# Keys and values by seven quarter products in the middle groups of a gated decoder, and one buffer for the turned rows

## The chip, the cores and the metric

The kernel runs on one core of one Trainium2 chip. The metric is the device time of one execution in microseconds; the figure for the kernel before is the median of three runs. Everything is fp32.

## What is computed

Four batches (NB = 4) of 512 rows of 512 numbers go through two layers. Each layer adds a gated cross attention and a gated feed-forward part to x. The part that matters here is the cross attention of the second layer, cut from the reference:

```python
x = x + jnp.tanh(g_xattn[1]) * _L1_xattn_ref(_layernorm(x, axis=-1), ctx_1024, Wq, Wk, Wv, Wo, gq, gk)
# _L1_xattn_ref: 16 heads of D = 128, context of 512 rows of 256 numbers per batch
q = rmsnorm((hidden_states @ Wq).reshape(B, Sq, H, D), gq)
k = rmsnorm((encoder_hidden_states @ Wk).reshape(B, Skv, H, D), gk)
v = (encoder_hidden_states @ Wv).reshape(B, Skv, H, D)
attn = softmax(einsum('bqhd,bkhd->bhqk', q, k) / sqrt(D))
out = einsum('bhqk,bkhd->bqhd', attn, v).reshape(B, Sq, H * D) @ Wo
```

The first layer has another cross attention and a linear layer. The feed-forward part of the second layer is a mixture of 16 experts, applied to the first batch alone.

## The kernel before

**Groups and steps.** The second layer's attention is cut into 32 groups of two heads (G = 2), eight for each batch. `groups[m]` is the batch and the pair of group m. `step(i)` does head i of 64, so a group is two steps: h = 0 and h = 1. A step has four quarters. Each quarter starts with one score matmul (`scores(i, quarter)`, bank psS), and then issues what the lists `pieces` and `extra` hold for it. Group m's steps also make the keys, values and queries of group q = m + 1, and multiply the finished values and the output projection of earlier heads.

**The order of the work.** It is written out by hand. Each engine runs its instructions in the order in which the program issues them. `later(n, f)` puts f off until `tick` has counted n more units, where a 512-column matmul counts about one; so DVE and ACT work is issued between matmuls.

**Keys and values before.** `keys_values(q, chunks)` runs in the h = 0 step: in quarter 0 for two of four chunks of context rows, in quarter 1 for the other two. A chunk is two matmuls of 512 columns (keys and values of both heads side by side) into one bank psA, and ACT copies the halves to `kn` and `v`. Then, in the same function, come the squares of kn (ACT, L796), the mean and rsqrt (DVE L806, POOL L193), the scaling of kn (POOL L810), 32x32 transposes (DVE L821), and a way out to DRAM and back in another order (`k_d` L828 and `kT` L836), both issued on ACT's queue. `kT` is what the next group's first score matmul reads.

**Queries.** `queries` makes them by plain products (L858). For the groups `SWITCH[0] <= q < SWITCH[1]`, 12 to 27, `quarter_queries` makes them by seven products of quarters (L881): POOL combines the quarters of the weights (L731 to L734), and DVE the quarters of the turned rows once for a batch (`combine_rows`).

**Turned rows.** `turned_rows` gives the pieces that normalise a batch's rows (DVE, L227), transpose them on TensorE (L245, bank psT) and copy them to `lnT` (ACT, L250). For batches 1 to 3 its four statistics pieces start at step (b-1)*16 + 8, and its four turning pieces follow, one in quarter 3 of each of the next four steps. `lnT` has two buffers, which layer 0's `xTs` use as well.

**Beside it.** From step 22 on, the experts' blocks lie between the attention's pieces, one block for two steps: `rows_T` (L1133) in h = 0 quarter 0, the gate and up products (L1141) in quarters 1 and 2, and down (L1169) in h = 1 quarter 2. SP's queue loads all weights and moves the probabilities (`big<-tP`). The projections (L1066) and their adds to x (DVE L276) end a group. PSUM has eight banks: three psA, two psS, two psT, one psO.

Of the kernel before, what the change touches and what calls it, by code (L numbers as in the profile page):

```python
# [9 lines left out]
F32 = mybir.dt.float32  # L10
I32 = mybir.dt.int32
AF = mybir.ActivationFunctionType
ALU = mybir.AluOpType
AX = mybir.AxisListType

P = 128
NB = 4
S = 512
# [4 lines left out]
G = 2  # L23
NG = H // G
# [4 lines left out]
NC = S // P  # L29
KC = DM // P  # L30
# [3 lines left out]
SWITCH = (12, 28)  # L34
# [21 lines left out]
def tile_gated_decoder(  # L56
# [19 lines left out]
    nc = tc.nc  # L76
    const = ctx.enter_context(tc.tile_pool(name="const", bufs=1))
    work = ctx.enter_context(tc.tile_pool(name="work", bufs=2))
# [9 lines left out]
    def ps_a():  # L88
        return ps("psA", 3)
# [4 lines left out]
    def ps_t():  # L94
        return ps("psT", 2)
# [5 lines left out]
        return work.tile([P, 4, 512], F32, tag="big", bufs=2, name="big")  # L101

    def lnt():
        return work.tile([P, KC, S], F32, tag="lnT", bufs=2, name="lnT")

    def row(tag, bufs):
        return work.tile([P, 512], F32, tag=tag, bufs=bufs, name=tag)
# [10 lines left out]
    ctxs = {}  # L118
# [80 lines left out]
    def later(n, f):  # L199
        heapq.heappush(pending, (clock[0] + n, next(serial), f))  # L200

    def tick(n=1):
        clock[0] += n
        while pending and pending[0][0] <= clock[0]:
            heapq.heappop(pending)[2]()
# [138 lines left out]
    def l0_rows(b, c):  # L344

        if c == 0:
            xTs[b] = lnt()
        pt = ps_t()
        for k in range(KC):
            nc.tensor.transpose(  # L350
                pt[:, k * P : (k + 1) * P], x_sb[:, b * NC + c, k * P : (k + 1) * P], ident
            )
        later(0, lambda: nc.scalar.copy(
            xTs[b][:, :, c * P : (c + 1) * P], pt.rearrange("p (k q) -> p k q", k=KC)
        ))
        tick(0.5)
# [352 lines left out]

    HS, HK = S // 2, KC // 2

    def by_quarters(m):
        return SWITCH[0] <= m < SWITCH[1]
# [38 lines left out]
    def load_wo(m):  # L754
# [2 lines left out]
        nc.sync.dma_start(t, wo_v[:, g * G : (g + 1) * G, :])  # L757
        wo_of[m] = t

    def keys_values(m, chunks):  # L760


        b, wkv = groups[m][0], wkv_of[m]
        if m not in v_of:
            kn_of[m] = work.tile([P, NC, GD], F32, tag="kn", bufs=1, name="kn")
            v_of[m] = work.tile([P, NC, GD], F32, tag="v", bufs=3, name="v")
        kn, v = kn_of[m], v_of[m]

        def copies(c, pp):
            nc.scalar.copy(kn[:, c, :], pp[:, 0:GD])  # L770
            nc.scalar.copy(v[:, c, :], pp[:, GD : 2 * GD])  # L771

        for c in chunks:
            pp = ps_a()
            for k in range(CC):
                nc.tensor.matmul(  # L776
                    pp,
                    ctxs[b][:, k, c * P : (c + 1) * P],
                    wkv[:, k, :, :].rearrange("p a n -> p (a n)"),
                    start=(k == 0),  # L780
                    stop=(k == CC - 1),
                )
                tick()
            later(1, lambda c=c, pp=pp: copies(c, pp))
        if chunks[-1] < NC - 1:
            return
        st = {}

        def squares():
            st["kss"] = col(NC * G, "kss", 3)  # L790
            sq = work.tile([P, NC, GD], F32, tag="sq", bufs=1, name="ksq")

            def chunk(c):
                for h in range(G):
                    at = slice(h * D, (h + 1) * D)
                    nc.scalar.activation(  # L796
                        sq[:, c, at], kn[:, c, at], AF.Square,
                        accum_out=st["kss"][:, c * G + h : c * G + h + 1],
                    )

            for c in range(NC):
                later(c, lambda c=c: chunk(c))

        def scale():
            kss = st["kss"]
            nc.vector.tensor_scalar(kss, kss, 1.0 / D, EPS, ALU.mult, ALU.add)  # L806
            rk = col(NC * G, "rk", 3)
            rsqrt(rk, kss, NC * G)
            kn_v = kn.rearrange("p c (h d) -> p c h d", h=G)
            nc.gpsimd.tensor_tensor(  # L810
                kn_v, kn_v,
                rk.rearrange("p (c h) -> p c h", h=G).unsqueeze(3).broadcast_to([P, NC, G, D]),
                ALU.mult,
            )

        def turn():
            st["tK"] = work.tile([P, NT, G, NC, TB], F32, tag="tK", bufs=1, name="tK")
            for c in range(NC):  # L820
                nc.vector.transpose(  # L821
                    st["tK"][:, :, :, c, :].rearrange("p j h q -> p h j q"),
                    kn[:, c, :].rearrange("p (h j r) -> p h j r", h=G, r=TB),
                )

        def put_out():
            st["k_d"] = dram.tile([NT, TB, NT, G * P], F32, tag="k_d", bufs=2, name="k_d")
            nc.scalar.dma_start(  # L828
                st["k_d"].rearrange("t r j q -> (t r) (j q)"),
                st["tK"].rearrange("p j h c q -> p (j h c q)"),  # L830
            )

        def take_in():
            kT = work.tile([P, NT, G, P], F32, tag="kT", name="kT")
            for j in range(NT):
                nc.scalar.dma_start(  # L836
                    kT[j * TB : (j + 1) * TB].rearrange("r t h q -> r t (h q)"),
                    st["k_d"][:, :, j, :].rearrange("t r q -> r t q"),
                )
            k_of[m] = kT  # L840

        later(2, squares)
        later(6, scale)
        later(11, turn)
        later(14, put_out)
        later(18, take_in)
# [412 lines left out]
    def put(i, quarter, *fs):  # L1259
        extra.setdefault((i, quarter), []).extend(fs)  # L1260
# [19 lines left out]
    for b in range(1, NB):  # L1280
        i = (b - 1) * NG * G + NG
        for j, f in enumerate(turned_rows(b, lx1, lnt)):
            put(i + j // NC * (1 + j % NC), 3 if j >= NC else j, f)
        if (b + 1) * NG > SWITCH[0]:
            put(2 * max(b * NG, SWITCH[0]) - 2, 1, lambda b=b: combine_rows(b))
        if b > 1:
            put(i, 3, lambda b=b: load_ctx(b))

# [12 lines left out]
    def step(i):  # L1301
        m, h = divmod(i, G)
        q = m + 1
        late, late_before = by_quarters(q), by_quarters(m)
        pieces = [[], [], [], []]
        if i >= G:
            pieces[0 if i == n - 1 or h and late else 2].append(lambda: values(i - G))
        if i == n - 1:
            pieces[1].append(lambda: project(m - 1, [0, 1]))
            pieces[2] += [lambda: project(m - 1, [2, 3]), lambda: end_turn(0)]  # L1310
            pieces[3] += [lambda: values(i - 1), lambda: end_turn(1)]
            pieces[3] += [lambda: end_values(0), lambda: end_turn(2), lambda: end_values(1)]
            pieces[3] += [lambda: project(m, [0]), lambda: end_turn(3), lambda: end_values(2)]
            pieces[3] += [lambda: project(m, [1]), lambda: end_values(3)]
            pieces[3] += [lambda: project(m, [2]), lambda: project(m, [3])]
        if h == 0:
            if 0 < m < M - 1:
                pieces[0].append(lambda: keys_values(q, [0, 1]))
                pieces[1].append(lambda: keys_values(q, [2, 3]))
            if m + 2 < M:  # L1320
                pieces[2 if late else 3].append(lambda: load_wkv(m + 2))
            if m >= 2 and not late_before:
                pieces[3].append(lambda: project(m - 2, [2, 3]))
                pieces[3].append(lambda: later(4, lambda: load_wo(m)))
            if late and q < M:
                pieces[3].append(lambda: quarter_queries(q, 0))
        elif i < n - 1:
            if q < M and not late:
                pieces[0].append(lambda: queries(q, 0))
            if q < M:  # L1330
                pieces[1].append(lambda: (quarter_queries if late else queries)(q, 1))
            if m + 2 < M:
                pieces[2].append(lambda: later(6, load_wq(m + 2)))
            if late:
                pieces[2].append(lambda: project(m - 1, [0, 1]))
            if m >= 1:
                pieces[3].append(lambda: project(m - 1, [2, 3] if late else [0, 1]))
            if late and q < M:
                pieces[3].append(lambda: later(2, lambda: load_wo(q)))
            if m == 0:  # L1340
                pieces[3].append(lambda: tick(8))
        for quarter in range(4):
            if i < n:
                scores(i, quarter)
            more = extra.get((i, quarter), [])
            for f in more + pieces[quarter] if late and h and quarter == 2 else pieces[quarter] + more:
                f()
# [73 lines left out]
```

## Time and profile before

| | us |
|---|---|
| median of three runs | 1440.65 (1440.38 to 1442.33) |
| the profiled execution | 1437.51 |
| its span in the trace | 1435.7 |
| TensorE busy in it | 1408.4 |
| VectorE (DVE) busy | 936.2 |
| ScalarE (ACT) busy | 574.7 |
| GpSimd (POOL) busy | 332.9 |
| a group's length, groups 15 to 19 and 23 to 26 | 41.8 |

PE is TensorE's matmuls and PEld its weight loads, which overlap them. Busy time is the union of an engine's instructions. The profiled execution is one run; its own time stands against its span, and the runs' median stands about 3 us above it. A group's length is measured from its first score matmul to that of the next group.

### The profile page before, as it was taken

To read this page: it belongs to the slowest core of one execution; us is meant where nothing else is said; L and a number is where in the kernel's file an instruction comes from. 1 tells how busy PE (TensorE), PEld (TensorE's weight loads), DVE (VectorE), ACT (ScalarE), POOL (GpSimd) and SP (SyncE) were. 2 spreads that over 40 slices of the span, in tenths; PEclk is the share of its full clock that TensorE was granted. 3 is DMA by queue.
4 is the path that set the end of the run, shared out by engine and by line. 5 is a ranking of instruction groups with operands and counts; after the bars stand their busy time and mean duration, and the time that the engine had idled before them with its cause. 6 is when DMAs were issued, how large, how long until landed. Compare 5 with 4: busy or idle time off the path is not lost.

```text
span 1435.7 us, 14871 instructions
## 1 busy us (share of the span) xinstructions
PE 1408.4 (98%) x3937; PEld 703.1 (49%) x3937; DVE 936.2 (65%) x2216; ACT 574.7 (40%) x1708; POOL 332.9 (23%) x274
## 2 busy tenths in 40 slices
PE   8999998999999999999999999999999999999998
PEld 4554443444444444555555555554555555544434
DVE  4778766767666677655666655566656565667774
ACT  5652224444444444333443334344334344434431
POOL 2324315322111112212221212221221222012320
PEclk9999999999999999999999999999999999999999
DMA  7533026545444445455565665656565666555652
GB/s 258 175 127 123 1 66 181 147 138 136 132 133 140 133 143 172 154 170 177 173 168 174 205 210 147 187 174 178 176 188 151 191 205 183 162 154 167 194 148 83
DMA packets 155356, 226.99 MB, mean 158 GB/s; under 512 B 24576, under 2 KB 90640, under 8 KB 155264
## 3 DMA queue, kind: packets, MB, share of 16 engines
q1 hardware_dynamic: 127312, 177.86, 42.1%
q10 hardware_dynamic: 23040, 33.56, 7.3%
q0 software_dynamic: 4912, 14.53, 3.7%
q8 instruction: 35, 0.57, 0.2%
q14 instruction: 57, 0.47, 0.1%
HBM read 129.62 MB, written 30.17 MB: 111 GB/s over the span
## 4 chain that ended last, share of the span: by engine, by line
PE 82%; DVE 8%; ACT 3%; DMA 2%; issue 1%; POOL 1%; SPq 1%; ACTq 0%; POOLq 0%
PE psA L776 15%; PE psS L968 13%; PE psO L1015 13%; PE psA L858 7%; PE psA L1066 6%; PE psA L881 5%; PE psA L1141 5%; PE psT L1066 3%; PE psO L1066 3%; PE psA L364 3%; PE psA L1169 2%; PE psA L695 1%; DMA kT<-k_d 1%; DVE x_sb L276 1%; ACT prob L983 1%
## 5 line engine op out<-in xcount | busy, mean ns | idle before, releaser
L983 ACT ACTIVATE prob<-prob,top 128x512 f32<-128x512 f32 x256 | 184.6, 721 | 562.5 <-DVE prob L982 524.1
L968 PE MATMUL psS<-kT,qT 128*128 128x512 f32 x512 | 262.3, 596 | 5.0 <-DVE x_sb L276 2.8
L776 PE MATMUL psA<-wkv,ctx 128*128 128x512 f32 x512 | 231.8, 593 | 0.3 <-ACT v L771 0.3
L1015 PE MATMUL psO<-big,v 128*128 128x512 f32 x504 | 228.9, 596 | 0.0
L982 DVE TENSOR_SCALAR_CACHE_REDUCE prob<-psS,rq 128x512 f32<-128x512 f32 x256 | 188.0, 736 | 28.9 <-PE psS L968 18.5
L989 DVE RECIPROCAL rden<-den 128x1 f32<-128x1 f32 x256 | 41.5, 162 | 242.2 <-ACT prob L983 232.9
L261 DVE STREAM_TRANSPOSE tP<-prob 128x512 f32<-128x512 f32 x252 | 178.7, 709 | 6.5
L193 POOL TENSOR_TENSOR rq<-qss,mhalf 128x8 f32<-128x8 f32 x32 | 53.4, 1668 | 485.3 <-DVE qss L955 485.3
L1015 PEld LDWEIGHTS psO<-big,v 128*128 128x128 f32 x504 | 96.0, 191 | 119.8 <-issue 115.5
L776 PEld LDWEIGHTS psA<-wkv,ctx 128*128 128x128 f32 x512 | 96.3, 190 | 118.1 <-issue 109.6
L990 DVE TENSOR_SCALAR prob<-prob,rden 128x512 f32<-128x512 f32 x256 | 141.3, 552 | 9.0
L968 PEld LDWEIGHTS psS<-kT,qT 128*128 128x128 f32 x512 | 92.9, 190 | 79.6 <-issue 62.0
L193 POOL TENSOR_TENSOR rk<-kss,mhalf 128x8 f32<-128x8 f32 x32 | 52.8, 1650 | 319.3 <-DVE kss L806 319.2
L1066 PE MATMUL psA<-wo,oT 128*128 128x512 f32 x256 | 121.1, 594 | 2.2 <-ACT oT L1022 2.2
L858 PE MATMUL psA<-lnT,wq 128*128 128x512 f32 x256 | 115.6, 592 | 0.0
L1141 PE MATMUL psA<-gu,xgT 128*128 128x352 f32 x272 | 86.0, 459 | 0.0
L821 DVE STREAM_TRANSPOSE tK<-kn 128x256 f32<-128x256 f32 x128 | 45.4, 411 | 55.3 <-POOL kn L810 55.3
L1066 PEld LDWEIGHTS psA<-wo,oT 128*128 128x128 f32 x256 | 48.1, 190 | 64.2 <-issue 54.4
L858 PEld LDWEIGHTS psA<-lnT,wq 128*128 128x128 f32 x256 | 48.3, 190 | 59.3 <-issue 59.3
L796 ACT ACTIVATE ksq<-kn 128x128 f32<-128x128 f32 x256 | 75.2, 298 | 0.0
L1141 PEld LDWEIGHTS psA<-gu,xgT 128*128 128x128 f32 x272 | 51.7, 190 | 37.9 <-issue 15.5
L276 DVE SCALAR_TENSOR_TENSOR x_sb<-psA,tg,x_sb 128x512 f32<-128x512 f32 x80 | 58.2, 727 | 6.7 <-PE psA L695 3.8
(197 smaller groups left out, 1811.5 us busy)
## 6 DMA issues: line engine op xcount, KB each, us to landing
big<-tP SPq DMA_DIRECT2D x1008, 64.0 KB
k_d<-tK ACTq DMA_DIRECT2D x32, 512.0 KB
kT<-k_d ACTq DMA_DIRECT2D x128, 128.0 KB
wq<-in_wq_dram SPq DMA_DIRECT2D x32, 512.0 KB
wo<-in_wo_dram SPq DMA_DIRECT2D x32, 512.0 KB
gu<-in_gate_dram SPq DMA_DIRECT2D x16, 704.0 KB
gu<-in_up_dram SPq DMA_DIRECT2D x16, 704.0 KB
wkv<-in_wk_dram SPq DMA_DIRECT2D x32, 256.0 KB
```

Of the source, the lines that this page charges most:

```text
L193: nc.gpsimd.tensor_tensor(out, v, mhalf[:, :n], ALU.pow)
L261: nc.vector.transpose(tP[:, :, c, :], e.rearrange("p (j r) -> p j r", r=TB))
L776: nc.tensor.matmul(pp, ctxs[b][:, k, c * P : (c + 1) * P], wkv[:, k, :, :].rearrange("p a n -> p (a n)"), start=(k == 0), stop=(k == CC - 1),)
L796: nc.scalar.activation(sq[:, c, at], kn[:, c, at], AF.Square, accum_out=st["kss"][:, c * G + h : c * G + h + 1],)
L858: nc.tensor.matmul(pp, wq[:, k, h * D : (h + 1) * D], lx1[b][:, k, :], start=(k == 0), stop=(k == KC - 1))
L968: nc.tensor.matmul(sc, q_of[m][h][:, c * P : (c + 1) * P], k_of[m][:, :, h, :], start=True, stop=True)
L982: nc.vector.tensor_scalar(e, x, scale, 3.0e38, ALU.mult, ALU.min, accum_out=top)
L983: nc.scalar.activation(st["e"], st["e"], AF.Exp, bias=top, scale=-1.0, accum_out=st["den"])
L990: nc.vector.tensor_scalar(st["e"], st["e"], rden, None, ALU.mult)
L1015: nc.tensor.matmul(po, v[:, k, h * D : (h + 1) * D], pT[:, :, k, :], start=(k == 0), stop=(k == NC - 1))
L1066: nc.tensor.matmul(pp, oT[:, j, c * P : (c + 1) * P], wo[:, j, :], start=(j == 0), stop=(j == G - 1))
L1141: nc.tensor.matmul(st[a][:, :FF], st["xgT"][:, k * P : (k + 1) * P], st["gu"][:, a, k, :], start=(k == 0), stop=(k == KC - 1),)
```

## The change

For the sixteen groups 12 to 27, keys and values are no longer made by `keys_values` but by `quarter_keys_values`. It treats the product of context and weights as a product of matrices of two by two quarters: the context's rows in two halves and its 256 inputs in two halves, the inputs and the outputs (keys, values) of the weights likewise. Seven products of quarters replace eight; each is two matmuls of 256 columns.

The sums of quarters are made on POOL: `combine_wkv` for each group's weights (in the h = 1 step two groups ahead), `combine_ctx` once for the context of batches 1 to 3. The products add up in three banks: px and py (psA) and pz (psT). px is used four times on top of itself, and ACT copies it out after each. DVE adds the other two banks to the copies. The calls are spread over quarters 0 to 2 of the h = 0 step: products 0, 1 and 4, then 5, then 6 ahead of the values, then 3 and 2 behind them. The keys' further way is the old one, moved into `turn_keys`, and it begins after the last product.

`lnT` gets one buffer instead of two. In layer 0 the odd batches' `xTs` get a buffer of their own. The four turning pieces of batches 1 to 3 move to the last quarters ahead of the batch's first queries: quarters 2 and 3 of step 16b-3, and 0 and 1 of step 16b-2. `combine_rows` moves from quarter 1 to quarter 2 of its step.

```diff
     def lnt():
-        return work.tile([P, KC, S], F32, tag="lnT", bufs=2, name="lnT")
+        return work.tile([P, KC, S], F32, tag="lnT", bufs=1, name="lnT")
...
         if c == 0:
-            xTs[b] = lnt()
+            xTs[b] = pool0.tile([P, KC, S], F32, tag="xT", bufs=1, name="xT") if b % 2 else lnt()
...
+    def combine_ctx(b):
+        t = ctxs[b]
+        sums = moe.tile([P, 4, HS], F32, tag="ctxs", bufs=1, name="ctxs")
+        a11, a12, a21, a22 = (t[:, a, c * HS : (c + 1) * HS] for c in (0, 1) for a in (0, 1))
+        s1, s2, s3, s4 = (sums[:, j] for j in range(4))
+        nc.gpsimd.tensor_tensor(s1, a21, a22, ALU.add)
+        nc.gpsimd.tensor_tensor(s3, a11, a21, ALU.subtract)
+        nc.gpsimd.tensor_tensor(s2, s1, a11, ALU.subtract)
+        nc.gpsimd.tensor_tensor(s4, a12, s2, ALU.subtract)
+        kv_ctx[b] = [a11, a12, s4, a22, s1, s2, s3]
+
+    def combine_wkv(m):
+        w = wkv_of[m]
+        sums = moe.tile([P, 3, GD], F32, tag="wkvs", bufs=1, name="wkvs")
+        b11, b12, b21, b22 = (w[:, a, c] for a in (0, 1) for c in (0, 1))
+        t1, t2, t4 = (sums[:, j] for j in range(3))
+        nc.gpsimd.tensor_tensor(t1, b12, b11, ALU.subtract)
+        nc.gpsimd.tensor_tensor(t2, b22, t1, ALU.subtract)
+        nc.gpsimd.tensor_tensor(b12, b22, b12, ALU.subtract)
+        nc.gpsimd.tensor_tensor(t4, b21, t2, ALU.subtract)
+        kv_w[m] = [b11, b21, b22, t4, t1, t2, b12]
+
+    def quarter_keys_values(m, part):
+        a, w = kv_ctx[groups[m][0]], kv_w[m]
+        if part == 0:
+            kn_of[m] = work.tile([P, NC, GD], F32, tag="kn", bufs=1, name="kn")
+            v_of[m] = work.tile([P, NC, GD], F32, tag="v", bufs=3, name="v")
+            kv_banks[m] = ps_a(), ps_a(), ps_t()
+        px, py, pz = kv_banks[m]
...
+        def product(j, out, start):
+            for t in (0, 1):
+                nc.tensor.matmul(
+                    out[:, t * GD : (t + 1) * GD], a[j][:, t * P : (t + 1) * P], w[j],
+                    start=start and t == 0, stop=True, skip_group_check=True,
+                )
+                tick(0.5)
+
+        if part == 0:
+            product(0, px, True)
+            later(0, lambda: nc.scalar.copy(k_lo, px))
+            product(1, py, True)
+            product(4, pz, True)
+            later(1, lambda: nc.vector.tensor_tensor(k_lo, py, k_lo, ALU.add))
+        elif part == 1:
+            product(5, px, False)
+            later(0, lambda: nc.scalar.copy(v_lo, px))
+        elif part == 2:
+            product(6, px, False)
+
+            def third():
+                nc.scalar.copy(v_hi, px)
+                nc.vector.tensor_tensor(v_hi, pz, v_hi, ALU.add)
+
+            later(0, third)
+        else:
+            product(3, px, False)
+            product(2, pz, False)
+
+            def last():
+                nc.scalar.copy(k_hi, px)
+                nc.vector.tensor_tensor(v_lo, pz, v_lo, ALU.add)
+
+            later(0, last)
+            turn_keys(m)
...
         for j, f in enumerate(turned_rows(b, lx1, lnt)):
-            put(i + j // NC * (1 + j % NC), 3 if j >= NC else j, f)
+            at = i * NC + j if j < NC else (b * NG * G - 3) * NC + 2 + j - NC
+            put(at // NC, at % NC, f)
         if (b + 1) * NG > SWITCH[0]:
-            put(2 * max(b * NG, SWITCH[0]) - 2, 1, lambda b=b: combine_rows(b))
+            put(2 * max(b * NG, SWITCH[0]) - 2, 2, lambda b=b: later(1, lambda: combine_rows(b)))
+            put(2 * max(b * NG, SWITCH[0]) - 3, 1, lambda b=b: combine_ctx(b))
...
-            if 0 < m < M - 1:
+            if late and 0 < m < M - 1:
+                for j in (0, 1):
+                    pieces[j].append(lambda j=j: quarter_keys_values(q, j))
+                pieces[2] = [lambda: quarter_keys_values(q, 2)] + pieces[2]
+                pieces[2].append(lambda: quarter_keys_values(q, 3))
+            elif 0 < m < M - 1:
                 pieces[0].append(lambda: keys_values(q, [0, 1]))
                 pieces[1].append(lambda: keys_values(q, [2, 3]))
...
+            if m + 2 < M and by_quarters(m + 2):
+                pieces[0].append(lambda: combine_wkv(m + 2))
```

More of the change, by code (lines that the diff above doesn't have):

```diff
@@ L758, in load_wo @@
         wo_of[m] = t
+    kv_ctx, kv_w, kv_banks = {}, {}, {}
+    def combine_ctx(b):
[8 more added lines that the diff above has]
+        kv_ctx[b] = [a11, a12, s4, a22, s1, s2, s3]
@@ new lines, in quarter_keys_values @@
+    def quarter_keys_values(m, part):
[5 more added lines that the diff above has]
+        px, py, pz = kv_banks[m]
+        k_lo, k_hi, v_lo, v_hi = (
+            t[:, c : c + 2, :].rearrange("p c n -> p (c n)") for t in (kn_of[m], v_of[m]) for c in (0, 2)
+        )
[4 more added lines that the diff above has]
+                    start=start and t == 0, stop=True, skip_group_check=True,
+                )
+                tick(0.5)
[22 more added lines that the diff above has]
+            turn_keys(m)
@@ L784, in keys_values, with turn_keys @@
             later(1, lambda c=c, pp=pp: copies(c, pp))
-        if chunks[-1] < NC - 1:
-            return
-        st = {}
+        if chunks[-1] == NC - 1:
+            turn_keys(m)
+    def turn_keys(m):
+        kn, st = kn_of[m], {}
         def squares():
```

## The prediction, made before the changed kernel ran

> **What bounds the kernel now.** I read the page first: TensorE (PE) is busy 98% of the span, at full granted clock in every slice, 82% of the chain that ended last is PE, and the key and value products (L776, 16% of PE's time) wait 0.3 us in all.
>
> ```profile
> PE 1408.4 (98%) x3937; PEld 703.1 (49%) x3937; DVE 936.2 (65%) x2216; ACT 574.7 (40%) x1708; POOL 332.9 (23%) x274
> ...
> PEclk9999999999999999999999999999999999999999
> ...
> PE 82%; DVE 8%; ACT 3%; DMA 2%; issue 1%; POOL 1%; SPq 1%; ACTq 0%; POOLq 0%
> ...
> L776 PE MATMUL psA<-wkv,ctx 128*128 128x512 f32 x512 | 231.8, 593 | 0.3 <-ACT v L771 0.3
> ```
>
> An average says little about a stage, so next I cut the middle groups into their lengths (start of one group's first score matmul to the next one's). With group m = 18 as an example, 860.8 to 902.6, PE has no gap at all; the last row also shows where the DMA engines are full.
>
> ```profile
> 860.80:866.80 6.00, 6.00 (x18) 2.86 (x17) 4.80 (x11) 2.42 (x7) 2.82 (x4) 1.00 0.35 98
> ...
> 896.80:902.60 5.80, 5.80 (x16) 2.69 (x15) 4.37 (x11) 1.23 (x4) 1.68 (x1) 1.00 0.97 335
> sum 41.80, PE 41.80 PEld 22.55 DVE 25.14 ACT 16.72 POOL 9.09; mean PE 5.97 PEld 3.22 DVE 3.59 ACT 2.39 POOL 1.30
> ```
>
> (Columns: length, then PE, PEld, DVE, ACT, POOL busy with counts, clock, DMA share, GB/s.) So in this stage a microsecond taken from PE is a microsecond of time, as long as nobody makes PE wait. The chain of waits over the same group has only PE pieces, among them
>
> ```profile
> 861.82 3.43 PE psA L776 x8
> ...
> 866.55 3.43 PE psA L776 x8
> ...
> 879.86 3.45 PE psA L881 x16
> ```
>
> Each fp32 matmul is two records. Eight records of 512 columns take 3.43 us (0.429 each), sixteen of 256 columns 3.45 (0.216 each).
>
> **Part 1, seven products.** Per group the old form is 8 matmuls, 16 records, 2 x 3.43 = 6.87 us. The new one is 7 x 2 matmuls of 256 columns, 28 records, 28 x 3.45/16 = 6.04 us. Saved 0.83 us a group, 16 groups: **-13.2 us**.
> A rule speaks against this. The Trainium skill (TensorE: Matmul & The Clock Gate, section "Back-to-back issue gap") says that the spacing of a real stream is set by weight load and matmul together, and that a narrow matmul costs more than its columns (about 81 against 56 ns at 128 columns). If I put those 25 ns, as an estimate, on each of the 28 narrow records, 0.7 of the 0.83 us would be gone and the part would be worth 2 us. The row decides: L881 already runs 256-column fp32 records with a fresh weight load (190 ns, shorter than 216) at exactly half the 512-column step. I take 0.83.
>
> **Part 2, what the other engines get, per group.** ACT loses eight 128x256 copies (371 and 381 ns, 3.0 us) and gains four 128x512 copies (583 ns as L1022, 2.3). DVE gains three 128x512 adds that read PSUM (L276: 727 ns), 2.2 us, 25.1 becoming 27.3 of 41. POOL gains four 128x256 sums (L731: 743 ns), 3.0 us, 9.1 becoming 12.1, and the same again once for each of three batches. They stand behind the keys' scaling on POOL, so the gather of the next block's rows, which is behind them, moves from t = 19 to about 29 (t counts from the group's first score matmul, 860.8 in the example); its reader is in the next group, at 44. These busy times cost nothing by themselves: no engine comes near 41 us. Moved transfers: none in number or size. What counts is order, and there are two new waits on the path.
>
> **Part 3, the wait inside the products.** The second product pair adds into the bank px that the first filled, so PE must wait until ACT has copied k_lo from px. On ACT that copy is queued behind the exponential of quarter 0, and that behind DVE's scaling of the scores, which comes late because DVE still adds the previous group's projections.
>
> ```profile
> 863.34 0.74 DVE L982 TENSOR_SCALAR_CACHE_REDUCE prob<-psS,rq 128x512 f32<-128x512 f32 x1
> ...
> 864.13 0.72 ACT L983 ACTIVATE prob<-prob,top 128x512 f32<-128x512 f32 x1 [3.46 <-DVE prob L982]
> ...
> 864.75 0.19 ACT L983 ACTIVATION_READ_ACCUMULATOR prob<-prob,top 128x1 f32 x1
> ...
> 864.85 0.35 ACT L770 COPY kn<-psA 128x256 f32<-128x256 f32 x1
> ```
>
> The copy would start there at t = 4.1 and end at 4.7. PE, unhindered: scores 0.86, three products 2.59, the block's row transposes 0.43, scores 0.86, so the pair is due at 4.74; its weights are loaded one step (0.43) ahead. A release at 4.7 therefore leaves a hole of about 0.3 us. The exponential of quarter 0 ends 4.1 to 5.0 after its matmul in the undisturbed groups (15 to 19 and 23 to 26), so the bounds are 0 and 1 us; I take 0.3 x 16 = **+4.8 us**. The later hand-overs (px after the next two copies, pz after the DVE add) have 0.4 to 1.5 us to spare by the same walk, since the block's hidden product (2.4 us) or the values (3.43) stand between. Behind PE's wait stands everything; behind DVE's new wait for the v_hi copy (1.5 us idle) stands only the share of quarter 2, whose rows are read two heads later.
>
> **Part 4, the keys are finished later.** Old: last kv matmul ends at t = 9.0, squares on ACT, rsqrt and scaling on POOL, transposes on DVE, then out to DRAM and back:
>
> ```profile
> 876.37 1.65 POOL L193 TENSOR_TENSOR rk<-kss,mhalf 128x8 f32<-128x8 f32 x1 [12.01 <-DVE kss L806]
> ...
> 880.03 1.42 DVE L821 STREAM_TRANSPOSE tK<-kn 128x256 f32<-128x256 f32 x4 [3.12 <-POOL kn L810]
> ...
> 882.57 0.34 ACTq L828 DMA_DIRECT2D k_d<-tK  x1
> ...
> 886.65 0.99 ACTq L836 DMA_DIRECT2D kT<-k_d  x2
> ...
> 888.37 2.37 ACTq L836 DMA_DIRECT2D kT<-k_d  x2
> ```
>
> Transposes at 19.2, out at 21.8, back at 25.9 to 29.9, landed about 31.6, used at 41.8: 10 us in hand. New: the products end at 14.9. k_hi copied 14.9, squares to 16.2, the exponential of quarter 3 to 20.1, other squares to 21.4, the query copy to 21.8, kss on DVE 22.4, POOL 24.1 and 26.1, transposes 26.2 to 27.7, out behind the exponential of quarter 5 at about 29.2, back behind the query scaling and the exponential of quarter 6 at about 34.4, that is 8.5 us later. The four issues then take 1.4 us if nothing holds them, and landing is 2 to 3 us after the last: 38 to 39 against a need at 40.5 (40.98 less the weight load).
> Two things crowd it. First, from t = 36 the next block's gate and up weights and the query weights (1.9 MB) fill the DMA engines (the 0.97 row above). The Trainium skill (DMA: Bandwidth & Descriptors, section "Queues, rings and completion order") says each engine goes round the queues it has work for, packet by packet; then 0.5 MB that needs about 2 us alone (its shares in the trace sum to 1.9) takes about 4, and lands at 39 to 40.5. Served behind what is queued before it, it would land at 41.5 or later. No undisturbed group of the trace has both at once, so the ends are 0 and 1.5 us a group. Second, ACT stands still while an issue waits:
>
> ```profile
> ACT hT L1162 <- DMA kT<-k_d: 37.4, 10, 5.0
> ```
>
> Behind it now stand the exponentials of quarter 7 and of the next group's quarter 0, and so part 3's copy. I take the half share, 0.15 us a group: **+2.4 us**.
>
> **Part 5, the turned rows.** They leave groups 12 to 14 and 20 to 22. Those are 43.6, 43.9, 43.4 and 43.1, 43.6, 43.9 us long against 41.8: 10.6 us over, of which eight turns of 0.44 are the transposes themselves; 7 us are stalls. The statistics stay, so some stall stays: I count 5.5 freed. They come back around groups 14/15 and 22/23: two scalings (0.64 each) ahead of quarter 0 on DVE lengthen part 3's hole to about 1.3 us, the four sums of combine_rows (about 0.7 each) now end about 1.1 us after the second query product wants its operand, where they were long done before, and they push the keys 2.4 us later: about 3.3 us at each border, 6.6. The first batch's turn moves into groups 6 and 7, whose keys have 3.5 and 4.7 us in hand: +1. Net **+2.1**, ends -5 and +10. Giving odd batches their own xT in layer 0 only renames a buffer: its reader has ended before it is written again, 0.
>
> **Sum:** -13.2 + 4.8 + 2.4 + 2.1 = -3.9; the bounds are -18 and +37 if every one fell the same way. The profiled execution took 1437.5 (span 1435.7 and 1.8 around it), 3.1 below the median of 1440.65; the difference is put on the median: **1436.7 us**.
>
> **Rivals.** (a) *No new wait bites:* part 3's copy comes before the weight load because DVE is less behind (with the keys' issues moved, quarters 5 and 6 are no longer held on ACT), and the keys land in time. For it: the hidden slack of 10 us, and PE's lack of gaps. Then only -13.2 and about +1 from the rows: 1428.5. (b) *The keys land late in every group, and it gets slower:* kT shares the full DMA stretch and lands at t = 42 instead of 40. PE waits about 1.2 us at the head of each of 16 groups, +19; with parts 3 and 5 the sum is -13.2 + 4.8 + 19 + 2.1 = +12.7: 1453. It decides from 0.4 us of lateness a group (the 6.3 us that parts 1, 3 and 5 leave over, by 16), which is a landing at about t = 41. For it: the full stretch; against: four transfers of 128 KB on 16 engines that go round. (c) *The products are not cheaper* (the rule of part 1): 1440.65 - 2 + 9 = 1448; the L881 row excludes it almost.
>
> **Numbers.** This kernel can be told from no change by about 0.2%, 2.9 us, so faster is below 1437.8. Chances: the forecast's own case, waits partly paid, 0.42 (1432 to 1440: two thirds faster, one third same); rival a 0.27; rival b 0.28 (mostly above 1443.5); rival c 0.03. That gives faster 0.55, same 0.14, slower 0.31. The range runs from just under rival a, 1426, to 1450, which is 1 us of lateness a group.
>
> **What would show it.** Right: the keys' and values' records at 0.216 in the middle groups; lengths near 41.3; new PE waits on ACT's kn copy of 0.2 to 0.5 us. Wrong upward: PE's scores waiting for DMA kT, groups over 41.8 with DMA share 1.0 ahead of them. Wrong downward: groups of 41.0 and no gap. Part 5 is wrong if groups 12 to 14 keep their length, or 15 and 23 are over 45.

## The result, and the profile after

The changed kernel takes 1455.12 us (median of four runs, 1453.61 to 1456.91). The kernel before took 1440.52 beside it. The ratio is 1.0101, with a 95% interval of 1.0083 to 1.0118: the change makes the kernel 1% slower. The prediction was 1436.7 with a range to 1450, so both the sign and the range are wrong. What happened is rival (b), which was priced at 1453.

The page of the kernel after:

```profile
span 1454.4 us, 15357 instructions
...
PE 1401.2 (96%) x4129; PEld 740.4 (51%) x4129; DVE 975.6 (67%) x2264; ACT 573.5 (39%) x1644; POOL 391.1 (27%) x350
...
PE 65%; DMA 11%; SPq 10%; DVE 8%; issue 3%; ACT 2%; POOL 1%; ACTq 0%; POOLq 0%
...
L1045 PE MATMUL psS<-kT,qT 128*128 128x512 f32 x512 | 265.3, 602 | 28.4 <-DMA kT<-k_d 18.5
```

TensorE's busy time fell by 7 us, and yet the span grew by 18.7. In the chain that ended last, PE's share fell from 82 to 65%, and DMA went from 2 to 11%. TensorE now stands idle for 28.4 us ahead of the scores, mostly for `kT`; before, it was 5.0:

```profile
L968 PE MATMUL psS<-kT,qT 128*128 128x512 f32 x512 | 262.3, 596 | 5.0 <-DVE x_sb L276 2.8
```

TensorE's waits in the kernel after say the same, in sum, times and longest one:

```profile
PE psS L1045 <- DMA kT<-k_d: 18.5, 12, 2.8
PE psS L1045 <- issue: 8.1, 4, 3.0
...
PE psA L958 <- DVE lxs L751: 1.8, 2, 0.9
...
PE psA L800 <- POOL wq L734: 1.7, 1, 1.7
PE psA L1143 <- DVE qT L992: 1.4, 1, 1.4
...
PE psA L800 <- ACT kn L808: 1.1, 1, 1.1
```

The second line belongs to the first. Of the 12 and 4 waits fifteen stand at the heads of groups 13 to 27, 25.6 us in sum; the sixteenth, 0.95 us, is at the head of group 2, where the kernel before waits too (2.1 us). The last line is the wait that part 3 had priced at 4.8 us; it bit once. The chain through one group (m = 17, 828.0 to 871.7; start, duration, what) shows how it comes about:

```profile
829.09 1.73 PE psA L800 x8
...
845.46 0.86 PE psS L1045 x2
846.31 3.45 PE psA L958 x16
849.77 0.87 PE psS L1045 x2
...
858.59 3.93 DMA big<-tP
862.52 0.02 issue
862.54 7.67 DMA kT<-k_d
870.21 1.46 issue
871.66 1.33 PE psS L1045 x2
```

Eight records of the new products (L800) take 1.73 us, 0.216 each, as part 1 said. The chain then leaves TensorE at 850.6, runs along SP's issues of the probabilities' moves (left out here), and ends in a transfer of `kT` that is on its way for 7.67 us. Before, the example group of the prediction had only PE pieces. In the last 3.7 us TensorE runs dry while the DMA engines are full, and afterwards its granted clock (the column ahead of the DMA share) is 0.60 and 0.55 in two rows, a loss of 0.8 and 0.9 us:

```profile
868.00:870.00 2.00, 1.22 (x3) 0.19 (x1) 1.97 (x4) 0.00 (x0) 0.00 (x0) 1.00 1.08 275
870.00:872.00 2.00, 0.34 (x1) 0.30 (x2) 0.43 (x1) 0.00 (x0) 0.00 (x0) 1.00 1.05 338
872.00:874.00 2.00, 2.00 (x5) 1.19 (x4) 0.76 (x2) 0.09 (x1) 0.86 (x2) 0.60 0.39 112
874.00:876.00 2.00, 2.00 (x6) 1.54 (x5) 1.17 (x3) 1.31 (x3) 2.00 (x3) 0.55 0.42 102
876.00:878.00 2.00, 2.00 (x11) 1.53 (x10) 0.98 (x2) 0.49 (x1) 0.14 (x1) 1.00 0.41 98
```

**Where the time went.** Groups 11 to 26 grew from 683.0 to 705.8 us in the profiled executions, 22.8 more; the groups ahead of them got 0.9 shorter and the tail 3.3. Of the 22.8, the products are -13.2 (16 x 0.83). TensorE's idle time in the last 4 us ahead of each group head (4.00 less its busy time, groups 13 to 27) sums to 25.5. After three of these holes the clock halved for about 3.4 us, which costs 1.7 each, 5.1 in all. What is left, about 5.4, is the border work of part 5 and everything else together. Group 11 alone, the first that makes the new products, grew by 2.7 us; TensorE waits in it 1.7 us for POOL's sums of weights (the profile names `wq`) and 1.4 until DVE has read the queries (`qT`), which the prediction did not price.

### The profile page after: what moved, and what is told of

It reads as the page before. It is cut to its first block, busy times and chain, and to the rows that moved or that the text cites. A ratio compares the mean times of both kernels' runs of the same rounds, so it can differ in the third digit from the quotient of the medians.

```text
span 1454.4 us, 15357 instructions
## 1 busy us (share of the span) xinstructions
PE 1401.2 (96%) x4129; PEld 740.4 (51%) x4129; DVE 975.6 (67%) x2264; ACT 573.5 (39%) x1644; POOL 391.1 (27%) x350
## 4 chain that ended last, share of the span: by engine, by line
PE 65%; DMA 11%; SPq 10%; DVE 8%; issue 3%; ACT 2%; POOL 1%; ACTq 0%; POOLq 0%
PE psS L1045 11%; PE psO L1092 10%; SPq L269 10%; DMA kT<-k_d 7%; PE psA L850 7%; PE psA L935 6%; PE psA L1218 6%; PE psA L800 5%; DMA big<-tP 3%; PE psA L958 3%; PE psA L1143 3%; PE psA L364 3%; PE psT L800 2%; PE psT L1143 2%; PE psO L1143 2%
## 5 line engine op out<-in xcount | busy, mean ns | idle before, releaser
L1045 PE MATMUL psS<-kT,qT 128*128 128x512 f32 x512 | 265.3, 602 | 28.4 <-DMA kT<-k_d 18.5
L1067 DVE TENSOR_SCALAR prob<-prob,rden 128x512 f32<-128x512 f32 x256 | 149.9, 585 | 9.0
L850 PE MATMUL psA<-wkv,ctx 128*128 128x512 f32 x256 | 116.0, 593 | 0.3 <-ACT v L845 0.3
L850 PEld LDWEIGHTS psA<-wkv,ctx 128*128 128x128 f32 x256 | 48.0, 190 | 58.6 <-issue 55.5
L887 POOL TENSOR_TENSOR kn<-kn,rk 128x1024 f32<-128x1024 f32 x32 | 61.4, 1919 | 2.5
```

The lines of the kernel that those rows point to most:

```text
L850: nc.tensor.matmul(pp, ctxs[b][:, k, c * P : (c + 1) * P], wkv[:, k, :, :].rearrange("p a n -> p (a n)"), start=(k == 0), stop=(k == CC - 1),)
L1045: nc.tensor.matmul(sc, q_of[m][h][:, c * P : (c + 1) * P], k_of[m][:, :, h, :], start=True, stop=True)
L1067: nc.vector.tensor_scalar(st["e"], st["e"], rden, None, ALU.mult)
```

## The experiments

The times in the table are medians over the runs of each kernel. They come from several chips, so kernels are compared by the ratio, which is to the kernel before on the same chip. "Calm groups" are 16 to 19 and 24 to 26, those without statistics or turning, with the means of their length, of the last `kT` issue and of the landing of `kT`, both from the group's first score matmul. "Landed" is the end of `kT`'s last packet. Where the next score matmul waited for it in the kernel after, it started another 0.5 to 1.1 us later, so at a group of 41.0 a landing past some 40 to 40.5 costs time. "In front" is what the SP queue had issued of gate, up and query weights ahead of the keys' last transfer, with the loads' sizes of 0.7 MB for gate, 0.7 for up and 0.5 for the query weights.

| kernel | us | ratio (95%) | calm group | last issue | landed | in front |
|---|---|---|---|---|---|---|
| before | 1440.52 | 1 | 41.81 | 30.0 | 31.6 | 0 |
| after | 1455.12 | 1.0101 (1.0083 to 1.0118) | 43.14 | 35.9 | 42.4 | all, 1.9 |
| e1, gate and up early | 1428.04 | 0.9947 (0.9926 to 0.9968) | 41.00 | 35.2 | 39.1 | query, 0.5 |
| e4, up early | 1454.56 | 1.0123 (1.0100 to 1.0146) | 42.99 | 35.9 | 42.3 | gate and query, 1.2 |
| e10, up early, query late | 1440.36 | 1.0022 (1.0009 to 1.0036) | 41.41 | 35.4 | 40.1 | gate, 0.7 |
| e12, query late | 1453.99 | 1.0118 (1.0080 to 1.0155) | 43.06 | 36.0 | 42.3 | gate and up, 1.4 |
| e7, products packed | 1483.38 | 1.0320 (1.0297 to 1.0343) | 44.00 | 34.0 | 35.6 | 0 |
| e9, packed, rows forward | 1471.25 | 1.0241 (1.0221 to 1.0260) | 44.13 | 34.1 | 35.8 | 0 |
| e2, rows alone | 1446.61 | 1.0060 (1.0040 to 1.0080) | 41.81 | 29.9 | 31.5 | 0 |
| e6, rows alone, gate and up early | 1441.78 | 1.0035 (1.0020 to 1.0050) | 41.81 | 28.9 | 31.0 | 0 |
| e5, before, gate and up early | 1431.42 | 0.9958 (0.9939 to 0.9977) | 41.81 | 29.0 | 31.2 | 0 |
| e13, before, both loads moved | 1431.42 | 0.9958 (0.9946 to 0.9970) | 41.81 | 28.9 | 31.1 | 0 |
| e8, e1 with rows forward | 1425.40 | 0.9923 (0.9905 to 0.9941) | 40.99 | 35.1 | 39.0 | query, 0.5 |
| e11, e8 with query late | 1421.71 | 0.9902 (0.9882 to 0.9922) | 40.99 | 35.3 | 36.9 | 0 |

### Is it the weights' loads? e1 and its control e5

```diff
-            work_of[0, 3] = [lambda: load_hidden(then)]
+            work_of[0, 2].append(lambda: load_hidden(then))
```

This moves the issue of gate and up from about t = 33 to 17.4 (t from the group's first score matmul), into a stretch in which the DMA engines were nearly idle (group 17 of the kernel after: DMA shares of 0.27, 0.04 and 0.00 in the three stretches of 2 us from 845 to 851). In e1 it is done to the kernel after, in e5 to the kernel before.

> The changed kernel, with the next block's gate and up weights (1.4 MB) issued one quarter earlier, so that they stand on SP's queue ahead of the probabilities' move and not behind it. Theory (the keys' transfer back lands late because it shares full DMA engines with these weights): the four kT issues stay at about t = 32 to 35 of a group, but land about 2 us after the last one, at 37 to 38 instead of 41.7; PE's wait for kT is gone, groups are 41.0 to 41.4 us instead of 42.4 to 44.4, and the kernel takes 1422 to 1432 us. Rival (the chain of squares, scaling and transposes is itself too long, the transfer is not slowed): landing stays at 41 or later, and the time within 4 us of 1455.

> Control: the kernel before with the gate and up weights issued one quarter earlier. Its keys land 10 us ahead of their use and PE has no gap in these groups, so both theories expect no change: 1437.5 to 1443.5. If it is faster by more than that, the earlier weights help by themselves, and that much has to be taken off what they bring to the changed kernel.

e1: 1428.0, as expected. The keys' chain is nearly the same (k_d at 28.5, last issue at 35.2 instead of 35.9), but the landing is 3.3 us earlier, at 39.1 (37 to 38 was expected). The waits on `kT` fall from 18.5 and 8.1 us to the following, of which the longest is the one at group 2:

```profile
PE psS L1045 <- DMA kT<-k_d: 5.5, 3, 2.5
```

and a calm group, 818.9 to 859.9, has no hole:

```profile
818.90:859.90 41.00, 41.00 (x137) 24.88 (x136) 27.65 (x65) 16.50 (x48) 11.65 (x12) 1.00 0.65 194
```

So the changed kernel without the late transfer is faster than before. e5 was expected to show no change and missed: it is 0.4% faster as well. Its groups 12, 13, 20 and 21 are 5.1 us shorter in sum (174.2 to 169.1), so a part of the stalls around the rows' statistics came from the late loads too, which the prediction had put on the turning: TensorE's waits in these four groups before, 2.5 us for ACT's copies `hT` and 1.7 for normalised rows, are gone. e1 less e5 is only 0.1%: with the loads out of the way, products and rows together are nearly worth nothing, which the next pair takes apart.

### What are the products and the rows worth? e2 and e6

e2 keeps the rows' move and the single buffer and makes keys and values by the old eight matmuls in all groups; e6 is the same with gate and up early. The opposite, products without the rows' move, needs two turned-row buffers and was not tried.

```diff
-            if late and 0 < m < M - 1:
+            if False:
...
-            if m + 2 < M and by_quarters(m + 2):
-                pieces[0].append(lambda: combine_wkv(m + 2))
```

> The changed kernel with the keys and values of all groups made by the old 512-column products: only the move of the turned rows, the single lnT buffer and the later combine_rows are left of the change. If the rows' move is near neutral (prediction: 5.5 us freed in groups 12 to 14 and 20 to 22, some 3 us each given back at the two borders, 1 at the first): 1434 to 1443, with groups 12 to 14 near 42.3, and groups 15 and 23 at 42.7 to 45. Rival (the rows' move is a main cause of the loss): over 1446.

> The rows' move alone (eight old matmuls a group for keys and values) with the next block's gate and up weights loaded one quarter earlier. Beside e1 it differs only in the seven products, so e1 less this one is what the products are worth once the keys' way is free of the weights. If the product's saving is whole (0.83 us a group by the records, and 0.8 more at each border because the keys' work stands less in front of combine_rows), this kernel is 13 to 18 us over e1: 1441 to 1446. If the waits inside the products ate half of it, 1434 to 1437. The early load itself should help the rows-alone kernel by at most the stalls left in groups 12 and 20, 0 to 5 us.

e2 missed its range of 1434 to 1443. The rows' move alone costs 0.6%, 8.6 us, where the prediction had 2.1. With the early loads it is e6 against e5, 0.77% or 11 us. The products are e1 against e6: 0.88% of 1436, **12.6 us**, just under the lower edge of what was expected, and beside part 1's 13.2. That the two come so near is partly chance. In the profiled executions the seven calm groups are 0.8 us shorter each, as part 1 says; but groups 11, 12 and 20 are 5.3 us longer with the products, and groups 15 and 23 and the tail 8.2 shorter. Where the rows' cost lies, TensorE's waits of e2 show in the first line, and the chain through group 15 shows the reason:

```profile
PE psA L958 <- DVE lxs L751: 5.5, 2, 2.8
PE psT L245 <- DVE y L227: 5.4, 5, 1.8
```

```profile
750.68 1.91 POOL kn L887
...
752.61 1.42 DVE tK L898 x4
754.04 0.41 DVE hh L1232
754.44 0.60 DVE lxs L749
755.04 0.61 DVE lxs L750
755.66 0.02 issue
755.68 0.70 DVE lxs L751
756.38 0.14 issue
756.52 4.43 PE psA L958 x12
...
766.43 2.59 PE psA L958 x12
```

DVE gets to the sums of `combine_rows` (L749 to L752) only after the keys' transposes (L898), and these wait for POOL. TensorE's query products (L958) stand 2.8 us for them, and then take 4.43 us for twelve records; ten microseconds later twelve of the same take 2.59. The clock was halved during the first twelve:

```profile
754.00:756.00 2.00, 0.00 (x0) 0.00 (x0) 1.97 (x5) 0.00 (x0) 0.00 (x0) 1.00 0.45 131
756.00:758.00 2.00, 1.48 (x4) 1.24 (x5) 1.73 (x4) 0.20 (x1) 0.00 (x0) 0.59 0.00 0
758.00:760.00 2.00, 2.00 (x7) 1.60 (x6) 1.32 (x4) 0.97 (x3) 0.00 (x0) 0.56 0.28 115
```

The four border groups 14, 15, 22 and 23 are 184.1 us long, 16.8 over four calm ones. The parts add up: transposes 3.5 (8 x 0.44), two holes on `lxs` 5.5, two on a normalised row 3.6, two halved clocks 3.4, in all 16.0. In the kernel after, the same wait is only 0.9 us a border; there the keys' transposes are issued later and no longer stand ahead of the sums.

### How much must stand in front? e4, e10 and e12

e4 moves only the up weights: `load_hidden` keeps those, and a new `load_gate` has the gate's.

```diff
-            work_of[0, 3] = [lambda: load_hidden(then)]
+            work_of[0, 2].append(lambda: load_hidden(then))
+            work_of[0, 3] = [lambda: load_gate(then)]
```

> The changed kernel, with only the up weights (0.7 MB, half of the two) issued one quarter earlier; the gate weights stay where they are. Theory of the shared DMA engines: the full stretch is shorter by 0.7 MB at some 380 GB/s, about 1.9 us, so kT lands near 40 and the groups are about 41.0 to 42.0 us long: 1428 to 1442, between the other two. Rival of the long chain: within 4 us of 1455.

Missed: with 0.7 MB less in front, `kT` landed no earlier (42.3). So e10 takes the query weights away as well, and e12 those alone, from the kernel after:

```diff
-                pieces[2].append(lambda: later(6, load_wq(m + 2)))
+                pieces[3 if late else 2].append(lambda: later(6, load_wq(m + 2)))
```

> e4 (up weights early, gate weights late) with the query weights of the group after next put one quarter later too, which by the order of the sync queue takes them behind the next group's first moves: in front of the keys' landing then stand 0.7 MB (gate) instead of 1.2. Theory (the keys' packets get through only when what was queued before them is done, so what counts is how many bytes stand there): kT lands 1.5 us earlier than in e4, near 39.5 to 40, and most of the wait on kT goes: 1430 to 1442. Rival (e4 missed for another reason, for instance the later two issues standing behind the exponentials): kT still lands past 41 and the time stays within 4 us of e4's 1455. A mishap of its own: the query weights, later, may hold the query products of quarter 3; the waits of TensorE on wq tell that apart.

> The changed kernel with only the query weights (0.5 MB) put behind the next group's first moves; gate and up (1.4 MB) stay where they are. The keys' issue is the same, 32 to 35.5. Theory (bytes queued in front): gate and up still hold the keys until about 40, kT lands near 41 to 42 instead of 42 to 42.6, groups 0.5 to 1 us shorter: 1440 to 1450. Rival (the query weights, issued last, are what the keys lose to): kT lands under 40 and the time falls to 1428 to 1436.

The expectations place the query weights wrongly: in the trace they are issued at 36.8, not in the next group, but that is behind the keys' last issue (35.4 to 36.0), which is what counts. e10: `kT` lands at 40.1 and the time falls by 1% against e4, as expected, though 11 us of waits on `kT` remain in the middle groups. e12 missed: no change, where 5 to 15 us were expected. The packets of one group tell why. In kB started per microsecond, the columns told apart by queue and packet size; left the kernel after (group 17), right e10 (group 18):

```
       after                          e10
 t   kT   gate, up   query      kT   gate, up   query
33   65       0         0        92       0        0
34  177      10         0       114      11        0
35   15     122         0        33      86        0
36    5     269         0        22     297        0
37    0     311         0       101     259        0
38   18     346         0        99      35        0
39   89     203         0        36      28       95
40  109     127        35        28       4      285
41   39      44       198         0       0      102
42    7      10       232         0       0       37
```

The first two of the keys' four transfers are issued ahead of the weights (32.2 and 32.8) and pass. The last two are issued at 34.5 and 35.0, behind gate and up (33.2 and 33.9). From t = 36 to 38 they get 23 of 949 kB, 2.4%, and move only as the weights run down. Group 17 is near the low end: counted over 3 us from 0.6 us after the end of the last issue, the calm groups give `kT` 2 to 11% of the bytes, and the middle groups as a whole up to 20%. The query weights, issued behind gate and up on the same queue, come after `kT` anyway. This is why taking them away leaves the kernel after as it was (e12), while in e4, where they stand right behind the gate weights, they flow at t = 37 to 40 together with `kT` (in group 18 of it 486 kB of theirs beside 247 of `kT`). Bytes alone do not order the cases exactly (1.2 MB in e4 held as long as 1.9), and why is open.

### Finish the keys earlier instead? e7 and e9

e7 leaves all loads where they were in the order of the work, and puts the seven products into the first two quarters: 0, 1, 4 and then 5 in quarter 0, 6 and then 3, 2 in quarter 1.

```diff
-                    pieces[j].append(lambda j=j: quarter_keys_values(q, j))
-                pieces[2] = [lambda: quarter_keys_values(q, 2)] + pieces[2]
-                pieces[2].append(lambda: quarter_keys_values(q, 3))
+                    pieces[j].append(lambda j=j: quarter_keys_values(q, 2 * j))
+                    behind[j].append(lambda j=j: quarter_keys_values(q, 2 * j + 1))
```

(`behind` holds what a quarter issues last.)

> The changed kernel with the weights' loads where they are, but the seven products packed into the first two quarters of the head, as the old matmuls were, so that the last one ends near t = 9.5 instead of 14.9. Theory (the keys are finished 5 us later, so their way back from DRAM runs into the weights): transposes near 19 to 20, the last issue near 30, kT landed near 32, no wait on kT, groups near 41.0 to 41.4, which gives 1426 to 1436. Rival (the weights' loads delay the keys wherever they stand, or the four-quarter order is not what is late): kT still lands past 40 and the time stays over 1448. A second rival: with the products close together TensorE waits for ACT's copies out of px, 0.3 to 0.6 us at each of two hand-overs, 10 to 19 us over the groups: 1438 to 1448 with kT in time.

Half of it holds. The keys do escape: their last issue, at 34.0, comes ahead of the gate weights' (36.0), `kT` lands at 35.6, 8 us ahead of its use, and no line of TensorE's waits names it. But the second rival came, and larger than it was priced, at 3.2% over the kernel before. A calm group is 44.0 us long with 41.7 of work. TensorE's largest waits:

```profile
PE psA L800 <- ACT kn L808: 22.7, 13, 2.1
PE psA L1143 <- DVE qT L992: 14.6, 15, 2.7
PE psT L245 <- DVE y L227: 7.2, 5, 2.8
```

The first is part 3's wait, 1.7 us each. The scaled scores of quarter 0 come 3.7 us after the start of their matmul here, against 1.2 in the kernel after, so the copy out of px comes late behind the exponential. In the second a projection waits until DVE has read the queries (`qT`). The spread over three quarters, which makes the keys late, is thus what keeps TensorE from waiting for the copies.

e9 adds e8's row order (next section) to e7.

> e7 (products packed, loads where they were) with e8's rows. If both reasons are right and independent: e7 less 3 to 6 us. If e7's products wait for ACT's copies, the rows change only the borders, and the difference to e7 is still that of e8 to e1.

It gains 0.8%, 11 us, over e7, more than the 3 to 6 expected: group 11 falls from 50.4 to 44.8, and 15 and 23 by 3.8 and 4.6. Groups 20 and 22 rise by 1.9 and 1.6, and the calm groups stay at 44.1.

### A better kernel: e8, e11, and e13 to compare it with

e8 is e1 with the turning pieces two to a quarter, and the sums that follow them earlier; for the first batch two groups earlier.

```diff
-            at = ... (b * NG * G - 3) * NC + 2 + j - NC
+            at = ... (b * NG * G - 3) * NC + 2 + (j - NC) // 2
...
-            put(2 * max(b * NG, SWITCH[0]) - 2, 2, lambda b=b: later(1, lambda: combine_rows(b)))
-            put(2 * max(b * NG, SWITCH[0]) - 3, 1, lambda b=b: combine_ctx(b))
+            put(2 * b * NG - 2 if b > 1 else 18, 0, lambda b=b: later(1, lambda: combine_rows(b)))
+            put(2 * b * NG - 3 if b > 1 else 17, 1, lambda b=b: combine_ctx(b))
```

e11 is e8 with e12's edit. e13 is the kernel before with both moves of loads.

> e1 with the border's work moved forward: the four normalise-and-turn pieces two to a quarter, so that combine_rows can go one to two quarters earlier, and the first batch's sums (rows and context) taken two groups before they are needed. Theory (combine_rows ends after the second query product wants it, and pushes the keys): groups 15 and 23 fall from 44.4 to 42.5 to 43.5, groups 11 and 12 by 1 to 2 us together, in all 3 to 6 us under e1: 1422 to 1425. Rival (what the border costs is the turning itself, on TensorE and ACT): same as e1 within 2 us, or worse, since four scalings now stand together on DVE in front of quarter 3.

> e8 (gate and up early, border's work forward) with the query weights behind the next group's first moves as well, so that nothing but the expert rows stands beside the keys. Theory: kT lands near 37 to 38 in every group, the waits on kT left in groups 12 and 20 (4.4 us in all) go, and nothing else changes: 1421 to 1424. Rival: the query weights come so late that POOL's sums of them hold the query products of quarter 3 or the keys' scaling behind them on POOL: slower than e8, 1428 or more, with waits of TensorE on wq or lxs.

> The kernel before the change with both moves of weights that helped the changed one: gate and up one quarter earlier, the query weights one quarter later. It tells how much of e11's gain is the loads' and how much the change's. In e5 (gate and up early alone) the keys had 9 us in hand in every group, so the query weights behind them should bring nothing more: ratio 0.994 to 0.998, groups at 41.81. If the product's 13 us less the rows' 10 us less what e8 won back is the change's own worth, e11 stands 5 to 10 us under this kernel. Rival (most of e11's gain is the loads'): this kernel comes within 3 us of e11, ratio 0.990 to 0.992.

e8 is 0.24% under e1, about at the expected edge; the two intervals overlap. Groups 11 and 12 fell from 91.2 to 87.8 in sum, 15 and 23 only from 44.4 to 43.8. Groups 14 and 22 rose by 0.5, and group 6, where the first turning now happens, by 1.7. The waits on `lxs` are gone, and TensorE waits for the turned copies instead. e11 came as expected: `kT` lands at 36.9, and groups 12, 13, 20 and 21, where the statistics make the keys late, fall from 169.1 to 164.3. A calm group there, and what is left of the waits (the one on `kT` is at group 2):

```profile
854.00:895.00 41.00, 41.00 (x137) 24.84 (x136) 27.64 (x66) 16.51 (x48) 12.50 (x13) 1.00 0.63 182
```

```profile
PE psT L800 <- ACT lnT L250: 3.6, 2, 1.9
...
PE psS L1045 <- DMA kT<-k_d: 1.1, 1, 1.1
```

At a ratio of 0.9902 it beats both kernels. e13 shows that the loads alone give 0.42%. The other 0.56%, 8 us, belong to the change and e8's order of the rows together; the change as it was written, with gate and up early, is only 0.1% ahead of e5.

## Why the prediction was wrong, step by step

**Part 1, the products (-13.2): right.** 0.216 us a record, a calm group of 40.99 to 41.00 without holes against 41.81, and 12.6 us between e1 and e6, partly by chance as said. The rule on narrow matmuls would have left 2 us; the row was the right choice.

**Part 2, the other engines: right.** DVE 27.65 us in a calm group of e1 (27.3 predicted), POOL 11.65 (12.1), ACT 16.5.

**Part 3, the wait for the copy (+4.8): not there.** 1.1 us once. The sum took DVE's lag at quarter 0 from the kernel before (2.5 us in the example). In the kernel after it is mostly 1.2, but there the late scores give DVE time to catch up; in e1, where nearly no score is late, it is 1.2 to 2.3 in all groups but one, and TensorE waits only 1.0 us once. So rival (a) was right about the lag; its reason for it, the earlier end of quarters 5 and 6 on ACT, was not tested. That the wait exists with a lag of 3.7, e7 shows.

**Part 4, the keys later (+2.4): this is the step that failed.** The walk through the engines was good: transposes 25.9 (26.2 predicted), k_d 28.6 (29.2), the last issue 35.9 (35.8 by the four issues from 34.4; the first came at 32.2). The failure is the landing. The forecast let `kT` share the DMA engines half and half with the weights, after the Trainium skill (DMA: Bandwidth & Descriptors, section "Queues, rings and completion order"), which has each engine go round the queues packet by packet. It then lands at 39 to 40.5. Measured were 2 to 11% of the bytes instead of a half over 3 us in the calm groups, and a landing at 42.4. In the calm groups the weights' issue (33.2 in group 17) came ahead of the last one or two of the four transfers. The other end in the text, "served behind what is queued before it, it would land at 41.5 or later", is nearer to what the packets show. Two more terms were left out. The score starts 0.5 to 1.1 us after the last packet, so the landing had to come by 39.9 to 40.5 and had less in hand than the sum gave it; and the upper price of "1.5 us a group" leaves out the clock. Rival (b) reached 1453 partly by luck, with 19 us for the lateness (here 25.5, and 5.1 of clock), 4.8 for part 3 that did not come, and 2.1 for rows that cost more. Its deciding point, a landing at about 41, was too late: e10 lands at 40.1 and is already 0.2% slower than before, with the dearer rows in it.

**Part 5, the turned rows (+2.1): mis-sized as well.** e2 measured 8.6 us, and e6 against e5 11. The term "about 3.3 us at each border" is about 8 in e2. It left out the holes for a normalised row, which add 3.6 us at the two borders, and the halved clock after the hole on `lxs`, 3.4. The term "5.5 freed" was wrong too: e2, in its profiled execution, shortens groups 12, 13, 20 and 21 by 1.8 only, and e5 shortens them by 5.1 without moving a row.

**Chances.** Rival (b) had 0.28. The text itself pointed at what was needed to weigh it higher: two transfers, full DMA engines, and no group in the trace with both at once. A landing estimated within 0.5 us of its need, on an assumption about sharing that no row showed, should not have been the likeliest case.

## What to carry to other kernels

When a change moves a round trip through DRAM later, list what other transfers are issued in the microseconds ahead of it, and reckon with its being served behind them, as here; a slack of 10 us was used up by 5.9 of later issue and 5 of slower transfer. Then the cheapest cure may be to move the other transfer: one move of the weight loads turned a loss of 1.0% into a gain of 0.5%. Give the old kernel the same move before crediting the change: it gained 0.4% by it. A saving in matmuls shows in the time only where no hole opens, and a hole can cost more than its length: in e2 a halved clock added 1.7 us to one of 1.90.

## What the runs showed of the hardware

**Order of service between DMA queues.** The keys' transfers on ACT's queue, issued about 1 us behind 1.4 MB on SP's queue, got 2.4% of the bytes for 3 us in the group shown and 2 to 11% in the calm groups; those issued ahead of it passed. In the two groups shown, service went nearly by the order of issue, across queues; what in the DMA engines makes it so is not shown. With nothing in front, landing came 1.6 us after the last issue (e11); behind gate and up it came 6.5 after.

**TensorE's clock.** After some holes the granted clock is 0.5 for about 3.4 us, which adds about 1.7. In the kernel after, it followed holes of 2.44, 2.59 and 2.99 us, but not one of 2.77; in e2 it followed one of 1.90, in e7 it left out one of 3.39, and no hole up to 1.89 in these three kernels was followed by it. The Trainium skill (TensorE: Matmul & The Clock Gate, section "HAM oscillation — how this bites in real kernels") warns of gaps over about 3.4 us; here gaps well under that were enough in some cases, so the rule does not hold here as it stands, and length alone does not tell which.
